# Ten gate buffers, all gates fetched within their step, and TensorE's block limits four instructions later

## The chip, the cores and the metric

The kernel runs on one core of a Trainium2 chip. Its five engines each work through a queue of their own in order: TensorE (PE, with weight loads listed apart as PEld), VectorE (DVE), ScalarE (ACT), GpSimd (POOL), and SyncE (SP), which here does nothing but issue DMAs. [...] The metric is the device time of one execution in microseconds (us); lower is better.

## The reference

One layer on an image x of shape (2, 128, 256, 256), all in float32: halo attention over windows, then a mixture of experts for each pixel, each with a normalisation before it and a residual around it.

```python
x = x + conv_attention(ln_over_channels(x))   # q, k, v by W_qkv; 8x8 windows look at 12x12 keys,
                                              # only every second row and column of them counts
t = tokens(x)
h = ln(t)
p = softmax(h @ router_w + router_b)          # 8 experts
top_p, top_i = top_k(p, 2); top_p /= top_p.sum()
out = einsum(h, expert_w) + expert_b          # all 8 experts
x = image(t + sum over the 2 chosen of top_p * out[top_i])
```

## The kernel before

**Steps.** The image is cut into strips of 8 rows, 32 a picture, 64 in all. The mask leaves only keys of one parity, so a strip falls into four planes (row parity by column parity) that attend separately. Each of the 256 planes is one step `n` of the loop at the end of the kernel; strip `i` and plane `pl` come from `divmod(n, 4)`. Seven more steps drain the pipeline. The scheduler's own ordering is off there: instructions run on each engine in the order in which the loop writes them, and generators (`score`, `attn`, `ahead`, `norm`, `outp`, `rout`) are advanced by `next` to interleave stages.

**What a step does.** It attends plane `n` (`scores` L462, `attend` L503, `out_project` L546), projects plane `n + 1` (`project` L400), and, a strip behind, runs the experts on 512 pixels. The experts are themselves spread over three steps: in one step the norms and the router of a group of pixels are computed; in the next its gates are written to DRAM (`spread` L648: gT to gd) and fetched back, each broadcast over 128 partitions; in the one after that they are multiplied in and the products made. `new` is the group whose gates are fetched in this step, `nxt` the one multiplied, `ex` the one whose products finish.

**Gates.** For each expert `e`, `fetch(e, eng)` (L680) takes a buffer `gb` of 128 x 512 from a ring, lets the engine `eng` touch its first column (a memset on DVE, L688, or a copy on ACT, L686), and issues the DMA on SP (L689). The touch makes one engine wait until the buffer's last reader is done, and the DMA then waits for that engine. `times(e, eng)` (L701, L705) multiplies the centred pixels `xs` by the gate into `xe`: 0 to 4 and 6 on DVE, 5 and 7 on POOL. `product(e)` (L711, L714) adds `xe` times the expert's weights into `acc`; `end` (L718, L720) adds `acc` to the pixels. `means` (L696, L699) makes `xs` from the pixels and `sb`, which `fetch_means` (L691, L694) brings.

**TensorE in a step**, in its order: 32 small matmuls with `keys` (L474) and 128 with `kcol` (L491), that is the scores; `pu` (L408), `pv` (L350), `pk` (L423), `pq` (L445) for the next plane; products of experts 4, 6, 7, 5 (L714, eight matmuls, since each product is two); 16 with `ones` (L512) and 128 with `vwin` (L522), that is the attention; the sums for the norms (L580, 32); products 0, 1, 2 (six matmuls), `po` (L550), product 3. Every matmul has a weight load, so that is 736 instructions. `pq` needs the PSUM buffer that `pu` had, which DVE frees with `uT` (L413).

**Alignment.** At the start of every full step TensorE gets an `addr_align` (L823): its next instruction is placed at `BLOCK - FIRST_LIMIT` = 161 in a block of 256 instructions, with no-ops as padding (they show on PEld's sequencer at L823, 32 a step). So the first block limit of a step comes 95 instructions after its start, and two more follow at every 256.

**SP in a step**, before: gates 5 and 7 of the group fetched in the step before (their touches on ACT), gd twice, vrows (values of the next plane, L369), rb (L665, the reciprocal deviation that `ln1` on POOL needs, L276), sb (L694), vwin in two halves (L381, `take_values`, which reads vrows back), gates 0, 1, 2, xt (L115, an image row pair ahead), gate 3, the output (L750, `store`), gate 4, the borders, gate 6.

**DVE in a step**: the router (L613 to L645), gT (L651), uT, the shifts (L392, L397), xs, six gate multiplications, `acc` to pixels (L720), sT, rc, rT, o for the attention (L532 to L542), the transposed sums plg (L589), the deviations (`rstd`, L232 to L239, with two activations on ACT between L235 and L238; then L596, L598), and `po` to pixels (L555). **POOL**: `behind` (L709, waits for DVE's last gate), gate 5, `ln1`, every fourth step `halo` (L250), gate 7.

Of the kernel before, what the change touches and what calls it, by code (L numbers as in the profile page):

```python
# [11 lines left out]
F32 = mybir.dt.float32  # L12
# [5 lines left out]
P = 128  # L18
# [25 lines left out]
KR, KC = 6, 10  # L44
NK = KR * KC
SLOT = 64
BLOCK, FIRST_LIMIT = 256, 95
NU = 9


# [1 line left out]
def kernel(  # L52
# [16 lines left out]
    nc = tc.nc  # L69
# [8 lines left out]
    NT = CH // P  # L78
# [7 lines left out]
    gates = ctx.enter_context(tc.tile_pool(name="gates", bufs=2))  # L86
# [18 lines left out]
    def load_x(i, k, paced=False):  # L105

        if i >= len(strips):
            return
        b, s = strips[i]
        if k == 0:  # L110
            xt[i] = xpool.tile([P, R, W], F32, tag="xt", name=f"xt{i}")
        r = s * R + 2 * k
        if paced:
            nc.scalar.copy(xt[i][:, 2 * k, 0:1], onesm[:, 0:1])
        nc.sync.dma_start(xt[i][:, 2 * k : 2 * k + 2, :], x[b, :, r : r + 2, :])  # L115
# [248 lines left out]
    def send_values(n, sent):  # L364

        i, pl = divmod(n, 4)
        for part, vr in sent:
            for k, at, m in runs(i, part):
                nc.sync.dma_start(  # L369
                    vrows[pl][1 : PC + 1, at : at + m, :],  # L370
                    vr[:, k - part[0] : k - part[0] + m],
                )

    def take_values(n):

        for half in range(2):
            src = vrows[n % 4][half * HP * 8 : half * HP * 8 + KC].rearrange("c r d -> (c r) d")
            src = src.unsqueeze(1)
            dims = [list(d) for d in src.ap]
            dims[1] = [8 * KR * P, HP]  # L380
            nc.sync.dma_start(  # L381
                vwin[n % 2][half * SLOT : half * SLOT + NK],
                bass.AP(src.tensor, src.offset, dims),
            )
# [77 lines left out]
    def scores(n, state):  # L462


        qs, kk, au = state["qs"], state["kk"], state["au"]
        turn = place(n // 4, 0) // 2
        att = ps_att.tile([P, 4, 512], F32, tag="att", name=f"att{n}")
        sc = att[:, :, 0:HQ]
        for w in range(2):
            for half in range(2):  # L470
                rows = slice(half * SLOT, (half + 1) * SLOT)
                for h in range(HEADS):
                    hp = slice(h * DH, (h + 1) * DH)
                    nc.tensor.matmul(  # L474
                        sc[rows, h].rearrange("p (t w z) -> p t w z", w=2, z=16)[:, :, w],
                        lhsT=keys[hp, turn, w],
                        rhs=au[hp, half * NP + w : (half + 1) * NP : 2].rearrange(
                            "p t a s -> p t (a s)"
                        ),
                        start=(w == 0),  # L480
                        stop=False,
                    )
        for t in range(HP):
            if t == HP // 2:
                yield
            for half in range(2):
                rows = slice(half * SLOT, (half + 1) * SLOT)
                m0 = 2 * (half * HP + t)
                for h in range(HEADS):
                    hp = slice(h * DH, (h + 1) * DH)  # L490
                    nc.tensor.matmul(  # L491
                        sc[rows, h, 32 * t : 32 * t + 32],
                        lhsT=kk[hp, half * HP + t, :],
                        rhs=qs[hp, m0 : m0 + 2].rearrange("p m a s -> p (m a s)"),
                        start=False,
                        stop=(t == HP - 1),
                    )
        pT = work.tile([P, HEADS, HQ], F32, tag="pT", name=f"pT{n}", bufs=1)
        nc.scalar.activation(pT, att[:, :, 0:HQ], AF.Exp)  # L499
        state.update(att=att, pT=pT)  # L500
        yield
# [166 lines left out]
    def to_all(gd, j):  # L668

        return gd[j * NT : (j + 1) * NT].rearrange("r k -> (r k)").partition_broadcast(P)  # L670

    class Experts:
# [7 lines left out]
        def fetch(self, e, eng):  # L680


            nm = "_".join(str(v) for v in (*self.at, e))
            self.gb[e] = gates.tile([P, NT * P], F32, tag="gb", name=f"gb{nm}", bufs=8)
            if eng is nc.scalar:
                eng.copy(self.gb[e][:, 0:1], onesm[:, 0:1])  # L686
            else:
                eng.memset(self.gb[e][:, 0:1], 0.0)  # L688
            nc.sync.dma_start(self.gb[e], to_all(self.gd, e))  # L689
# [55 lines left out]
    to_store = []  # L745

    def store(i, k):
        b, s = strips[i]
        r = s * R + 2 * k
        nc.sync.dma_start(out[b, :, r : r + 2, :], xt[i][:, 2 * k : 2 * k + 2, :])  # L750
        if k == R // 2 - 1:
            xt.pop(i)
# [4 lines left out]
    n_planes = 4 * len(strips)  # L757
# [45 lines left out]
    gated, ex, nxt = None, NoExperts(), NoExperts()  # L803
    last = ctile([P, 1], "last")
    pool, dve = nc.gpsimd, nc.vector

    ET = mybir.EngineType
    with tc.manual_schedule(engines={ET.PE, ET.DVE, ET.Activation, ET.Pool, ET.SP}):
        for n in range(n_planes + 7):
            i, pl = divmod(n, 4)  # L810
            score, attn, outp, ahead, norm, rout = none, none, none, none, none, none
            if n < n_planes:
                score = scores(n, states[n])
                attn = attend(n, states[n])
                outp = out_project(n, states[n])
            if n + 1 < n_planes:
                states[n + 1] = {}
                ahead = project(n + 1, states[n + 1])

            if 6 <= n < n_planes:
                nc.tensor.addr_align(BLOCK, offset=BLOCK - FIRST_LIMIT)  # L823


            next(score, None)
            new, row = NoExperts(), None
            if gated and gated[0]:
                rout = route(*gated[0], *gated[2])
            next(rout, None)  # L830
            nxt.fetch(5, nc.scalar)
            for _ in rout:
                pass
            next(score, None)
            next(ahead, None)
            nxt.fetch(7, nc.scalar)
            if gated:
                f, c, made = gated
                gd = spread(f, c, made[0], f"_{n}")
                new = Experts(*f, gd) if f else new  # L840
            if n + 1 < n_planes:
                send_values(n + 1, states[n + 1]["sent"])
            if gated and c:
                row = (*c, fetch_rstd(gd, f"_{n}"))
            next(ahead, None)
            if n + 1 < n_planes:
                states[n + 1]["shift"]()
            next(ahead, None)
            next(ahead, None)
            for e in (4, 6, 7, 5):  # L850
                ex.product(e)


            f = (i - 1, pl) if 0 < i <= len(strips) else None
            c = row_at(n)
            if f or c:
                norm = norms(f, c, f"_{n}")
            next(norm, None)
            next(attn, None)
            nxt.means()  # L860
            new.fetch_means()
            if n + 1 < n_planes:
                take_values(n + 1)
            for e in (0, 1, 2, 3):
                nxt.times(e, dve)
            new.fetch(0, dve)
            for e in (4, 6):
                nxt.times(e, dve)
            new.fetch(1, dve)
            ex.end()  # L870
            new.fetch(2, dve)
            next(attn, None)
            next(attn, None)


            ex = nxt
            next(norm, None)
            load_x((n + 9) // 4, (n + 9) % 4, paced=True)
            new.fetch(3, dve)
            while to_store:  # L880
                store(*to_store.pop())
            next(ahead, None)
            ex.product(0)
            made = next(norm, None)
            ex.product(1)
            ex.product(2)
            new.fetch(4, nc.scalar)
            nxt.behind(6)
            nxt.times(5, pool)
            if row:  # L890
                ln1(*row, pool)
            if pl == 3 and i + 2 < len(strips):
                halo(i + 2)
            nxt.times(7, pool)
            if n + 2 < n_planes:
                borders(n + 2)
            next(outp, None)
            ex.product(3)
            next(outp, None)
            new.fetch(6, dve)  # L900
            gated, nxt = (f, c, made) if made else None, new
            states.pop(n, None)

# [58 lines left out]
```

## Time and profile before

| What | us |
|---|---|
| median of 3 runs (lowest, highest) | 4416.81 (4413.12, 4420.5) |
| the profiled execution | 4415.92 |
| its span, first to last instruction | 4414.1 |
| start to the first of the 256 full steps | 29 |
| first steps with the experts not yet running | 114 (29 to 143) |
| steady steps | 4177 (143 to 4320) |
| draining steps | 94 (4320 to 4414) |
| TensorE busy in the steady part | 4084 of 4177, granted clock 1.00 |
| DVE busy in the steady part | 3700 |
| ACT, POOL busy in the steady part | 1399, 1055 |
| mean share of the 16 DMA engines in the steady part | 0.77 |

A line of the timeline has the start in us from the beginning of the span, the duration in us, the engine (with a q for its sequencer, which issues DMAs), the line of the kernel, the operation, what is written and read, the shape, and how many instructions were merged; in brackets stand the engine's idle time before the first of them and what ended it. "issue" there means that the engine waited for nothing that the profile shows. A line of the waits says who waited for whom: total in us, times, longest in us. A line of the windows begins with the stretch and its length, then busy us and instructions of PE, PEld, DVE, ACT and POOL, the granted TensorE clock, the share of the DMA engines and GB/s. A queue line has packets, MB and the share of 16 engines' time; q1 carries the kernel's transfers and q8 the instructions themselves. Matmuls are pipelined: a matmul of 512 columns is listed with some 0.6 us, but the next one starts 0.43 us after it, so starts are the better measure.

### The profile page before, as it was taken

What the parts mean: (1) busy time and instruction counts of PE and PEld (TensorE: products, weight loads), DVE (VectorE), ACT (ScalarE), POOL (GpSimd) and SP (SyncE); (2) the same over time, 40 slices, a digit from 0 to 9 for tenths busy, and PEclk for the clock granted to TensorE, in tenths of its full rate; (3) what the DMA queues carried; (4) which work ended last, traced back from release to release, by engine and by line L of the source; (5) the groups of instructions that cost most, each with busy time, mean ns of one, the idle gap of its engine ahead of it and who ended that gap; (6) DMA issues with size and microseconds to landing.
All of it is one profiled execution on the core that took longest, in us unless ns stands there. A gap on an engine that the chain in (4) does not pass through costs nothing. (4 is left out here: it accounts for less than half of the span.)

```text
span 4414.1 us, 224656 instructions
## 1 busy us (share of the span) xinstructions
PE 4254.2 (96%) x94273; PEld 2453.1 (56%) x94273; DVE 3844.2 (87%) x11850; ACT 1455.9 (33%) x3774; POOL 1092.5 (25%) x1126
## 2 busy tenths in 40 slices
PE   7899999999999999999999999999999999999987
PEld 4555555555555555555555555555555555555553
DVE  5788889888898988898888889988888888888877
ACT  3333333333333333333333333333333333333321
POOL 1122222222222222222222222222222222222211
PEclk9999999999999999999999999999999999999998
DMA  4677777777787777777878777777778777777865
GB/s 121 201 246 229 244 232 241 246 234 233 233 242 232 242 238 235 244 234 243 243 233 243 231 242 232 243 239 239 242 229 244 238 236 233 232 232 239 243 195 183
DMA packets 824580, 1022.19 MB, mean 232 GB/s; under 512 B 137634, under 2 KB 409634, under 8 KB 823594
## 3 DMA queue, kind: packets, MB, share of 16 engines
q1 hardware_dynamic: 822864, 1007.52, 74.6%
q8 instruction: 769, 12.60, 1.2%
q14 instruction: 217, 1.78, 0.1%
q10 hardware_dynamic: 730, 0.29, 0.0%
HBM read 863.78 MB, written 143.75 MB: 228 GB/s over the span
## 5 line engine op out<-in xcount | busy, mean ns | idle before, releaser
L714 PE MATMUL acc<-xe,ew 128*128 128x512 f32 x4096 | 1935.8, 602 | 66.7 <-issue 44.9
L714 PEld LDWEIGHTS acc<-xe,ew 128*128 128x128 f32 x4096 | 759.2, 190 | 1001.6 <-issue 931.2
L705 DVE TENSOR_TENSOR xe<-xs,gb 128x512 f32<-128x512 f32 x1536 | 951.0, 687 | 12.3 <-DMA gb<-gd 2.2
L709 POOL COPY last<-xe 128x1 f32<-128x1 f32 x256 | 47.0, 184 | 3119.1 <-DVE gb L688 3109.9
L705 POOL TENSOR_TENSOR xe<-xs,gb 128x512 f32<-128x512 f32 x512 | 650.8, 1272 | 2.5 <-PE acc L714 1.6
L276 POOL TENSOR_TENSOR xn<-xt,rb 128x512 f32<-128x512 f32 x249 | 374.0, 1502 | 171.5 <-DMA rb<-gd 165.4
L491 PE MATMUL att<-qs,kcol 32*64 32x32 f32 x32768 | 396.9, 226 | 4.8 <-issue 4.7
L491 PEld LDWEIGHTS att<-qs,kcol 32*64 32x64 f32 x32768 | 394.4, 131 | 6.3 <-issue 5.8
L522 PEld LDWEIGHTS att<-pT,vwin 64*32 64x32 f32 x32768 | 348.0, 105 | 37.5 <-issue 0.4
L522 PE MATMUL att<-pT,vwin 64*32 64x32 f32 x32768 | 343.3, 200 | 0.2 <-issue 0.2
L350 PEld LDWEIGHTS pv<-wt,xn 128*128 128x128 f32 x2048 | 270.5, 192 | 127.4 <-issue 80.1
L434 ACT COPY kcol<-pk 128x560 f32<-128x560 f32 (+2 forms) x344 | 318.9, 927 | 52.4 <-PE pk L423 49.0
L499 ACT ACTIVATE pT<-att 128x1024 f32<-128x1024 f32 x256 | 261.9, 1023 | 221.3 <-PE att L491 220.7
L532 DVE STREAM_TRANSPOSE sT<-att 128x512 f32<-128x512 f32 x256 | 183.5, 717 | 133.4 <-PE att L522 124.1
L445 PE MATMUL pq<-xn,wt 128*128 128x512 f32 x512 | 272.8, 614 | 23.4 <-DVE uT L413 21.4
L408 PE MATMUL pu<-xn,wrel 128*128 128x512 f32 x512 | 293.0, 654 | 0.0
L574 ACT ACTIVATE sq<-xt 128x512 f32<-128x512 f32 x505 | 291.8, 629 | 0.0
L397 DVE STREAM_TRANSPOSE au<-auT 128x512 f32<-128x512 f32 x256 | 272.5, 1064 | 9.0
L550 PE MATMUL po<-o,wt 128*128 128x512 f32 x512 | 265.1, 599 | 8.2 <-DVE o L542 5.8
L350 PE MATMUL pv<-wt,xn 128*128 128x128 f32 x2048 | 271.3, 275 | 0.9 <-issue 0.9
L423 PE MATMUL pk<-xn,wt 128*128 128x512 f32 (+2 forms) x528 | 263.4, 581 | 2.4 <-issue 1.3
L474 PEld LDWEIGHTS att<-au,keys 32*64 32x64 f32 x8192 | 117.2, 132 | 227.7 <-PE po L550 183.5
(2696 smaller groups left out, 4884.0 us busy)
## 6 DMA issues: line engine op xcount, KB each, us to landing
gb<-gd SPq DMA_DIRECT2D x2048, 256.0 KB, 5.7
vwin<-vrows SPq DMA_DIRECT2D x512, 240.0 KB, 5.4
xt<-in_x_dram SPq DMA_DIRECT2D x256, 256.0 KB, 6.4
sb<-gd SPq DMA_DIRECT2D x256, 256.0 KB, 4.2
out_dram<-xt SPq DMA_DIRECT2D x256, 256.0 KB, 6.0
rb<-gd SPq DMA_DIRECT2D x249, 256.0 KB, 3.4
vrows<-vr SPq DMA_DIRECT2D x168, 256.0 KB, 4.0
vrows<-vr SPq DMA_DIRECT2D x160, 128.0 KB, 3.6
```

Of the source, the lines that this page charges most:

```text
L276: eng.tensor_tensor(xn[i % 2][:, :, :, k, 1 : PC + 1], ln1_src(i, k).rearrange("p (y j x) -> p y x j", y=2, x=2), rb.rearrange("p (y j x) ...
L350: nc.tensor.matmul(pv[:, j * P : (j + 1) * P], lhsT=xp[:, k, 1 : PC + 1], rhs=wv, start=True, stop=True,)
L397: nc.vector.transpose(au.rearrange("p m a s -> p a s m"), auT[n % 2])
L408: nc.tensor.matmul(pu, lhsT=wrel, rhs=inner, start=True, stop=True)
L434: nc.scalar.copy(places[:, 1 : NP - 1], windows(new[:, :, KC - 3 :], 0, NP - 2))
L445: nc.tensor.matmul(pq, lhsT=wq, rhs=inner, start=True, stop=True)
L491: nc.tensor.matmul(sc[rows, h, 32 * t : 32 * t + 32], lhsT=kk[hp, half * HP + t, :], rhs=qs[hp, m0 : m0 + 2].rearrange("p m a s -> p (m a ...
L522: nc.tensor.matmul(av[hp, half, 32 * t : 32 * t + 32], lhsT=vv[rows, t, hp], rhs=pT[rows, h, 32 * t : 32 * t + 32], start=True, stop=True,)
L550: nc.tensor.matmul(po, lhsT=wo, rhs=state["o"].rearrange("p f z -> p (f z)"), start=True, stop=True)
L574: nc.scalar.activation(sq, src, AF.Square)
L705: eng.tensor_tensor(self.xe[e], self.xs, self.gb.pop(e), ALU.mult)
L714: nc.tensor.matmul(self.acc, lhsT=ew[:, e, :], rhs=self.xe.pop(e), start=(e == 0), stop=not self.xe)
```

## The change

Gates get ten buffers instead of eight. Gates 5 and 7, which were fetched at the beginning of the following step with touches on ACT, are fetched at the end of the step of their group, with touches on DVE, as is gate 4's; so all eight of a group are fetched in one step. The fetches, the two halves of `take_values`, the image load and the store are put in another order, and the first fetch comes after two gate multiplications rather than four. Gate 3's touch stands before the attention's transposes rather than after them. `FIRST_LIMIT` goes from 95 to 99, so TensorE's step starts at slot 157 of a block and each limit comes four instructions later in the step.

SP's order after it: gd twice, vrows, rb, sb, gate 0, vwin's first half, gate 1, xt, gate 2, gate 3, vwin's second half, the output, gates 4, 6, 5, 7, the borders.

```diff
--- before.py
+++ after.py
@@ -44,7 +44,7 @@
 KR, KC = 6, 10
 NK = KR * KC
 SLOT = 64
-BLOCK, FIRST_LIMIT = 256, 95
+BLOCK, FIRST_LIMIT = 256, 99
 NU = 9
 
 
@@ -371,9 +371,9 @@
                     vr[:, k - part[0] : k - part[0] + m],
                 )
 
-    def take_values(n):
-
-        for half in range(2):
+    def take_values(n, halves=(0, 1)):
+
+        for half in halves:
             src = vrows[n % 4][half * HP * 8 : half * HP * 8 + KC].rearrange("c r d -> (c r) d")
             src = src.unsqueeze(1)
             dims = [list(d) for d in src.ap]
@@ -681,7 +681,7 @@
 
 
             nm = "_".join(str(v) for v in (*self.at, e))
-            self.gb[e] = gates.tile([P, NT * P], F32, tag="gb", name=f"gb{nm}", bufs=8)
+            self.gb[e] = gates.tile([P, NT * P], F32, tag="gb", name=f"gb{nm}", bufs=10)
             if eng is nc.scalar:
                 eng.copy(self.gb[e][:, 0:1], onesm[:, 0:1])
             else:
@@ -828,12 +828,10 @@
             if gated and gated[0]:
                 rout = route(*gated[0], *gated[2])
             next(rout, None)
-            nxt.fetch(5, nc.scalar)
             for _ in rout:
                 pass
             next(score, None)
             next(ahead, None)
-            nxt.fetch(7, nc.scalar)
             if gated:
                 f, c, made = gated
                 gd = spread(f, c, made[0], f"_{n}")
@@ -859,32 +857,39 @@
             next(attn, None)
             nxt.means()
             new.fetch_means()
-            if n + 1 < n_planes:
-                take_values(n + 1)
-            for e in (0, 1, 2, 3):
+            for e in (0, 1):
                 nxt.times(e, dve)
             new.fetch(0, dve)
+            if n + 1 < n_planes:
+                take_values(n + 1, (0,))
+            for e in (2, 3):
+                nxt.times(e, dve)
+            new.fetch(1, dve)
+            load_x((n + 9) // 4, (n + 9) % 4, paced=True)
             for e in (4, 6):
                 nxt.times(e, dve)
-            new.fetch(1, dve)
+            new.fetch(2, dve)
             ex.end()
-            new.fetch(2, dve)
+            new.fetch(3, dve)
+            if n + 1 < n_planes:
+                take_values(n + 1, (1,))
+            while to_store:
+                store(*to_store.pop())
             next(attn, None)
+            new.fetch(4, dve)
             next(attn, None)
+            new.fetch(6, dve)
+            new.fetch(5, dve)
 
 
             ex = nxt
             next(norm, None)
-            load_x((n + 9) // 4, (n + 9) % 4, paced=True)
-            new.fetch(3, dve)
-            while to_store:
-                store(*to_store.pop())
             next(ahead, None)
             ex.product(0)
             made = next(norm, None)
+            new.fetch(7, dve)
             ex.product(1)
             ex.product(2)
-            new.fetch(4, nc.scalar)
             nxt.behind(6)
             nxt.times(5, pool)
             if row:
@@ -897,7 +902,6 @@
             next(outp, None)
             ex.product(3)
             next(outp, None)
-            new.fetch(6, dve)
             gated, nxt = (f, c, made) if made else None, new
             states.pop(n, None)
 
```

## The prediction

> **What bounds the kernel now.** I read the page first, then TensorE step by step in the timeline, the waits, the DMA queues, and at last the order in which SP issues.
>
> ```profile
> PE 4254.2 (96%) x94273; PEld 2453.1 (56%) x94273; DVE 3844.2 (87%) x11850; ACT 1455.9 (33%) x3774; POOL 1092.5 (25%) x1126
> ...
> q8 instruction: 769, 12.60, 1.2%
> ```
>
> TensorE is the bound. The 256 full steps (from one L474 to the next) take 16.80 us on average over steps 10 to 244. The fastest agree to the nanosecond, and there TensorE never pauses:
>
> ```profile
> 1620.10:1636.37 16.27, 16.27 (x370) 9.53 (x369) 14.67 (x44) 5.54 (x14) 4.71 (x5) 1.00 0.75 230
> ```
>
> So 0.52 us of a step, some 124 us over those 235 steps, is all that can be won from TensorE's pauses. Taking each matmul's start against the one before it, minus the usual spacing at its place in the step, puts them in four places: 62.3 us at the second matmul of L714's group of eight (101 steps), 45.5 us at L445 (pq), 7.5 us inside L491 (17 steps), 1.3 us inside L522. What ends the first two:
>
> ```profile
> 1155.28 0.59 PE L714 MATMUL acc<-xe,ew 128*128 128x512 f32 x1
> 1156.87 3.16 PE L714 MATMUL acc<-xe,ew 128*128 128x512 f32 x7 [1.00 <-issue]
> ...
> 1775.67 1.13 PE L445 MATMUL pq<-xn,wt 128*128 128x512 f32 x2 [0.42 <-DVE uT L413]
> ```
>
> The first is no wait on data. q8 brings 16 KB packets, three a step, and a step holds 768 TensorE instructions: a packet is a block of 256. Counting from the aligned start, the first limit falls 95 instructions in, at L491's 16th matmul (64 for L474, then 31). The second, at 351, is the second matmul of L714 (348 come before L714, then load, matmul, load). The third, at 607, is L522's 106th. These are exactly the places of the three pauses called "issue". Over 1154.4 to 1155.4 us the queues show
>
> ```profile
> q1 hardware_dynamic: 126, 0.22, 58.2%
> q8 instruction: 1, 0.02, 6.0%
> ```
>
> That packet starts at 1154.60, 4.1 us after the first limit was passed, and TensorE goes on 2.27 us after its start. No stalled step resumes sooner than 2.2 us after a packet's start. The packet for the second limit starts 3.1 us after the first limit in the median (2.2 to 4.2), and more DMAs in flight at that moment delay it: 2.70 us with four, 2.97 with five, 3.23 with six, 3.80 with seven, 0.37 us for each.
>
> SP shows why so much is in flight:
>
> ```profile
> 1150.89 3.88 SPq L689 DMA_DIRECT2D gb<-gd  x2
> 1154.87 1.71 SPq L659 DMA_DIRECT2D gd<-gT  x2
> 1156.63 1.05 SPq L369 DMA_DIRECT2D vrows<-vr  x2
> 1158.69 0.32 SPq L665 DMA_DIRECT2D rb<-gd  x1
> ```
>
> Gates 5 and 7 go out a step late, at 1.17 and 4.70 us after the step's start (medians), each behind an ACT copy, and SP's later issues queue behind them: gT is ready at 3.85, but gd leaves at 5.12.
>
> The pause at pq starts on DVE and POOL:
>
> ```profile
> 1768.49 0.99 DVE L235 SCALAR_TENSOR_TENSOR u__103_33034<-u__103_33034,epsc 128x8 f32<-128x8 f32 x1
> ...
> 1768.19 1.27 POOL L705 TENSOR_TENSOR xe<-xs,gb 128x512 f32<-128x512 f32 x1
> ...
> POOL xn L276 <- DMA rb<-gd: 165.4, 129, 29.2
> ```
>
> L235 usually takes 0.17 us. Here it ends 22 ns after POOL's multiplication, as in each of its 103 long cases. POOL is late because ln1 (L276) waits for rb. DVE is then late by 0.48 us on average in 122 such cases, uT has 0.25 us to spare (ends at 4.37, pq free at 4.66), and pq waits for the rest.
>
> **The change part by part.** FIRST_LIMIT 99 moves each limit four instructions: to L491's 18th matmul and L522's 108th (about 30 ns each), and to the fourth matmul of L714's group, two spacings of 0.43 later, 0.86 us. The padding stays within three blocks, so its no-ops cost what they cost now.
>
> *Second limit.* With every packet at its old time, only what exceeds 0.86 remains: 9.4 us in 25 steps, a gain of 53. The DMAs should also be earlier. From rb to the next step's drain there are fourteen transfers of about 256 KB at some 0.8 us each (4 MB in 12.5 busy us a step). They now start at 8.47 and saturate the engines to about 4 us of the next step. I expect rb at about 7.1 and the last gate at 16, so the backlog ends near 2 to 2.5, about two transfers less in flight at the first limit (0.7 us). I take a gain of 60. Bounds: 62, and 12 if instead two more are in flight.
>
> [...]
>
> *Third limit.* The stretch from the second limit to the third shrinks from 4.22 to 3.36 us, and the third packet starts 1.31 us after the second limit in the median (0.69 to 2.18), needing 2.2 more. If packets keep their absolute times, the pauses there grow from 1.3 to 6.2 us. If the packet moves the full 0.86 with the limit, they grow to 39.8 in 96 steps. Which? Where the previous packet came early, the next started as little as 0.02 us before the second limit's matmul, against 1.06 after it at least where that matmul had stalled: the sequencer runs up to 1.1 us ahead, which covers 0.86. I take a loss of 6; bounds 5 and 38.
>
> *First limit.* It moves 0.02 us and must be met within 4.2 us of the third. I take a gain of 2 from 7.5; bounds 7.5 gained and 10 lost, since SP now issues faster right after the third limit.
>
> *Gates, DVE and ACT.* Eight gates a step as before; three ACT copies of 0.18 us go (ACT is 33% busy, nothing on the path) and three DVE memsets of 59 ns come. A memset between two L705 costs nothing: 22 plus 579 ns from start to start against 602 without. Two come together after L542, and one now stands between L598 and L555; I allow 0.06 us, on the 0.25 spare. Gates 0 and 1 now reuse buffers that POOL read at 10.4 to 15.1 of the step before, so DVE finds them free at 7.7; the other six were last read by DVE earlier in its own queue. Behind these memsets stand sT and rstd: if one did wait, attention and then po would. Ten buffers cover the extra lifetime of two gates.
>
> *SP's queue.* Without gates 5 and 7 in front, gd leaves at about 4.0 instead of 5.12, vrows follow vr at 5.1 and rb goes at about 7.1 instead of 8.47. vwin's first half waits for vrows as now, but gate 0 passes it and fills the idle stretch before 10.5. The second half goes about 2 us later; it lands some 5.4 later, early in the next step, and L522 reads it at 9.5. xt moves ahead and still finds its ACT copy (7.75) done. The store finds L720 done at 10.9.
>
> *pq.* With rb earlier POOL ends at about 14.38, where L235 starts at 14.34, so most collisions go. In the quarter of steps with halo (L250, 0.62 us) POOL ends at 15.0: 62 times (0.70 minus 0.25) is 28 us. With 5 for the rest and 3 for the memsets, 45.5 becomes 36. Gain 10; bounds 30 gained, 15 lost.
>
> Sum: 60 - 6 + 2 + 10 = 66 us. The profiled execution took 4415.9 (span 4414.1, 1.8 around it), which gives 4349.9; the median shown is 0.9 higher, so **4350**. All pauses gone would be about 4298.
>
> **Rivals.**
> *The pause moves to the third limit (slower).* rb, sb and gate 0, now at 7 to 8.5 us, are in flight just when the third packet must start. It starts at 7.76 now; against the third limit at 10.67 it may start at 8.47. The other terms' gain of 72 is used up at 0.29 us a step, a start at 8.76. At 8.95 the pause is 0.48 in each of 245 steps, 118 lost against 72: 4462. For it: only 0.7 us of room. Against: the engines are only 38 to 69% busy at 5 to 7.5 now, and gate 7 leaves that stretch.
> *Half given back.* The packet does move with the limit (38 lost), rb comes no earlier (0), the second limit gains 53: 4402.
> *DVE becomes the bound.* Its work spaced back to back is 15.94 us a step, with collisions 16.20, against TensorE's 16.27. At 0.2 us for each of three memsets it is 16.80, today's step: 4417. Against: the free memset above.
> *It doesn't do what it says.* If the added waits change TensorE's count before L714, the limit doesn't land two matmuls on; only the DMA order acts, about 25 us: 4392.
>
> **How the numbers follow.** Forecast 0.58, half given back 0.15, limit misplaced 0.07, DVE bound 0.06, third limit 0.14. A difference under 0.2% (8.8 us) can't be told from none. The first three lie below 4408: faster 0.80; same 0.06; slower 0.14. The range 4300 to 4412 leaves out the slower case, most of the DVE case and a sliver below; the forecast's own range is 4300 to 4385.
>
> **What would show it.** Right: L714 in one piece of eight in most steps and pauses at its fourth matmul rare; q8's packets starting about 2 to 3 us after a step's start; gd right behind gT; POOL's wait for rb nearly gone; pq's waits only every fourth step. Wrong: an "issue" gap inside L522 in most steps, DVE memsets that wait, or a step floor other than 16.27.

## The result, and the profile after

| | us |
|---|---|
| before, median of the runs on the same chip (lowest, highest) | 4418.66 (4413.12, 4424.38) |
| after, median of 4 runs (lowest, highest) | 4632.52 (4620.21, 4636.44) |
| ratio after to before, with its 95% interval | 1.0479 (1.0455 to 1.0503) |
| span of the profiled execution, before and after | 4414.1 and 4630.3 |
| mean granted TensorE clock over the span, before and after | 0.992 and 0.980 |
| mean length of a step (steps 10 to 244), before and after | 16.80 and 17.68 |

The change made the kernel 4.8% slower; 4350 had been forecast, with a range up to 4412. The mean step is 0.885 us longer, which is 208 us over 235 steps, and nearly all of the 214 us between the medians.

The page after, engines and instruction queue:

```profile
PE 4311.1 (93%) x94273; PEld 2511.4 (54%) x94273; DVE 3816.6 (82%) x12618; ACT 1391.0 (30%) x3006; POOL 1089.4 (24%) x1126
...
q8 instruction: 769, 12.60, 1.2%
```

TensorE is still the bound, has the same 94273 matmuls and the same 769 packets of instructions, and the step without pauses is as long as before (the window line of one such step):

```profile
1622.27:1638.54 16.27, 16.27 (x369) 9.50 (x368) 14.76 (x50) 5.65 (x13) 4.67 (x5) 1.00 0.75 196
```

So neither DVE's three memsets nor more work on TensorE explains the loss: it lies in pauses. The waits after, for the places that mattered before (total us, times, longest us):

```profile
PE att L491 <- issue: 166.4, 175, 4.1
...
POOL xn L276 <- DMA rb<-gd: 114.0, 49, 30.4
...
PE att L522 <- issue: 48.4, 56, 1.9
...
PE acc L714 <- issue: 18.2, 34, 1.3
```

The pauses at L714 and at pq that the prediction set out to remove did shrink, and POOL waits less often for rb (49 times, 129 before). But L491, where the first limit of a step lies, now has the largest wait of TensorE's matmuls. Taking starts against starts as in the prediction (steps 10 to 244; us in total, with the number of steps over 30 ns; a matmul's usual spacing at its place is taken off):

| place | before | after | difference |
|---|---|---|---|
| first limit, in L491 | 7.5 (17) | 195.6 (191) | +188 |
| second limit, in L714 | 62.4 (101) | 25.3 (55) | -37 |
| third limit, in L522 | 1.3 (13) | 58.6 (87) | +57 |
| pq, L445 (both matmuls) | 45.5 | 6.6 | -39 |
| wider spacing at L408 and L350 | 1.1 | 39.3 | +38 |
| sum | | | +208 |

One step shows the first row. It starts at 1195.09. TensorE's timeline first, around the third limit, then around the first limit of the following step:

```profile
1205.89 1.15 PE L522 MATMUL att<-pT,vwin 64*32 64x32 f32 x107
1207.57 0.32 PE L522 MATMUL att<-pT,vwin 64*32 64x32 f32 x21 [0.53 <-issue]
...
1213.81 0.37 PE L491 MATMUL att<-qs,kcol 32*64 32x32 f32 x17
1215.50 1.34 PE L491 MATMUL att<-qs,kcol 32*64 32x32 f32 x111 [1.33 <-issue]
```

107 matmuls, then a pause, then 21: the third limit is at the 108th. 17 matmuls, then a pause, then 111: the first limit is at the 18th. Both are where the prediction's count puts them. SP's queue in the same stretch:

```profile
1201.94 0.35 SPq L665 DMA_DIRECT2D rb<-gd  x1
1202.42 0.37 SPq L694 DMA_DIRECT2D sb<-gd  x1
1203.62 0.32 SPq L689 DMA_DIRECT2D gb<-gd  x1
1204.43 0.34 SPq L381 DMA_DIRECT2D vwin<-vrows  x1
1204.86 0.39 SPq L689 DMA_DIRECT2D gb<-gd  x1
1205.31 1.28 SPq L115 DMA_DIRECT2D xt<-in_x_dram  x1
1206.64 0.90 SPq L689 DMA_DIRECT2D gb<-gd  x2
1207.64 0.39 SPq L381 DMA_DIRECT2D vwin<-vrows  x1
```

Eight transfers went out in the 5.6 us before the third limit (1207.57), six of them (four gates, half of vwin, xt) of the kind that went out at this limit or behind it before; the last line is already behind it. The instruction packet starts at 1212.96, 5.4 us after the limit; the queues from 1212.5 to 1213.5 are full:

```profile
q1 hardware_dynamic: 324, 0.31, 101.2%
q8 instruction: 1, 0.02, 6.1%
```

TensorE goes on 2.54 us after that packet's start; the shortest such time at any limit of steps 10 to 244 (without 123 to 130, which have other counts of matmuls) is 2.17 us here and was 2.18 before, the prediction's 2.2. Over all steps, the packet now starts 4.53 us after the third limit in the median, 2.19 before. It never starts sooner than 0.84 us after that limit in those steps before, 1.94 after; that it is asked for at the limit is read from these times. The first limit of the next step comes 6.45 us after the third (median before, from start to start), so by these numbers a packet that starts more than 6.45 less 2.2, that is 4.25 us, after the third limit should stop TensorE. It paused after 166 of the 167 packets that started later than that, and after 25 of the 67 others.

### The profile page after: what moved, and what is told of

Same layout as the page of the kernel before. It is cut to its first block, busy times and chain, and to the rows that moved or that the text cites. A ratio compares the mean times of both kernels' runs of the same rounds, so it can differ in the third digit from the quotient of the medians.

```text
span 4630.3 us, 224762 instructions
## 1 busy us (share of the span) xinstructions
PE 4311.1 (93%) x94273; PEld 2511.4 (54%) x94273; DVE 3816.6 (82%) x12618; ACT 1391.0 (30%) x3006; POOL 1089.4 (24%) x1126
## 3 DMA queue, kind: packets, MB, share of 16 engines
q1 hardware_dynamic: 822864, 1007.52, 75.6%
## 5 line engine op out<-in xcount | busy, mean ns | idle before, releaser
L714 PE MATMUL acc<-xe,ew 128*128 128x512 f32 x4096 | 1925.4, 601 | 36.9 <-issue 18.2
L714 PEld LDWEIGHTS acc<-xe,ew 128*128 128x128 f32 x4096 | 759.0, 190 | 965.4 <-issue 895.5
L491 PE MATMUL att<-qs,kcol 32*64 32x32 f32 x32768 | 433.3, 227 | 166.8 <-issue 166.4
L491 PEld LDWEIGHTS att<-qs,kcol 32*64 32x64 f32 x32768 | 413.8, 133 | 185.3 <-issue 184.1
L522 PEld LDWEIGHTS att<-pT,vwin 64*32 64x32 f32 x32768 | 351.1, 105 | 91.8 <-issue 54.5
L522 PE MATMUL att<-pT,vwin 64*32 64x32 f32 x32768 | 352.2, 200 | 48.8 <-issue 48.4
L350 PEld LDWEIGHTS pv<-wt,xn 128*128 128x128 f32 x2048 | 290.9, 205 | 141.0 <-issue 92.1
L408 PE MATMUL pu<-xn,wrel 128*128 128x512 f32 x512 | 315.7, 701 | 0.0
L413 DVE STREAM_TRANSPOSE uT<-pu 128x512 f32<-128x512 f32 x256 | 179.2, 700 | 146.6 <-PE pu L408 145.3
L350 PE MATMUL pv<-wt,xn 128*128 128x128 f32 x2048 | 289.2, 287 | 0.8 <-issue 0.8
L445 PE MATMUL pq<-xn,wt 128*128 128x512 f32 x512 | 263.2, 595 | 3.8 <-issue 2.3
```

The costliest lines, as they stand in the source:

```text
L350: nc.tensor.matmul(pv[:, j * P : (j + 1) * P], lhsT=xp[:, k, 1 : PC + 1], rhs=wv, start=True, stop=True,)
L408: nc.tensor.matmul(pu, lhsT=wrel, rhs=inner, start=True, stop=True)
L491: nc.tensor.matmul(sc[rows, h, 32 * t : 32 * t + 32], lhsT=kk[hp, half * HP + t, :], rhs=qs[hp, m0 : m0 + 2].rearrange("p m a s -> p (m a ...
L522: nc.tensor.matmul(av[hp, half, 32 * t : 32 * t + 32], lhsT=vv[rows, t, hp], rhs=pT[rows, h, 32 * t : 32 * t + 32], start=True, stop=True,)
L714: nc.tensor.matmul(self.acc, lhsT=ew[:, e, :], rhs=self.xe.pop(e), start=(e == 0), stop=not self.xe)
```

## The experiments

Each of them was also measured for its pauses (us as in the table above), for the median time from the third limit to the start of the packet, and for how many transfers SP issued in the 4 us before that limit. The times of e2, e3, e4, e5, e6, e8 and e9 are of one execution each, the others medians. The kernel before that ran beside them had a median of 4405.39 (e1, e2, e4, e6), 4418.88 (e3, e7, e8) or 4408.05 (e5, e9, e10).

| kernel | time | first | second | third | pq | packet after third limit | issued in 4 us |
|---|---|---|---|---|---|---|---|
| before | 4418.66 | 7.5 | 62.4 | 1.3 | 45.5 | 2.19 | 3.5 |
| after | 4632.52 | 195.6 | 25.3 | 58.6 | 6.6 | 4.53 | 5.6 |
| e1: limit 99 alone | 4374.84 | 13.4 | 8.2 | 19.5 | 44.4 | 2.18 | 3.5 |
| e2: after with limit 95 | 4631.62 | 176.2 | 78.4 | 42.2 | 1.4 | 4.53 | 5.8 |
| e4: five and seven in step | 4413.77 | 46.1 | 48.2 | 12.0 | 6.9 | 3.74 | 5.5 |
| e6: zero to three early | 4680.74 | 141.1 | 182.6 | 1.2 | 14.3 | 4.25 | 4.9 |
| e3: after, gates behind attention | 4540.28 | 128.7 | 62.8 | 16.1 | 11.4 | 4.03 | 3.9 |
| e8: after, values late | 4513.68 | 101.2 | 56.7 | 39.5 | 11.3 | 4.28 | 5.0 |
| e7: after, two gates then hold | 4425.24 | 43.9 | 49.8 | 15.5 | 27.0 | 3.95 | 4.0 |
| e5: before, gate 0 early | 4513.93 | 99.7 | 79.3 | 2.6 | 22.2 | 4.01 | 4.5 |
| e9: after, nothing in front | 4537.79 | 0.3 | 61.3 | 38.1 | 140.9 | 2.00 | 2.1 |
| e10: limit 99, gate 7 behind means | 4374.5 | 4.4 | 23.4 | 6.9 | 50.6 | 2.00 | 3.2 |

The theory after the result: the new order of SP's issues puts transfers in front of the third limit, the packet asked for there is served behind them, and TensorE stops at the next first limit. The rivals: the moved limit does it; more gates in flight from the end of the step do it.

**The limit alone (e1), and the order alone (e2).**

```diff
--- before                                   (e1)
-BLOCK, FIRST_LIMIT = 256, 95
+BLOCK, FIRST_LIMIT = 256, 99
--- after                                    (e2)
-BLOCK, FIRST_LIMIT = 256, 99
+BLOCK, FIRST_LIMIT = 256, 95
```

Of e1:

> The kernel before with FIRST_LIMIT 99 and nothing else. Theory (an instruction packet is served behind the transfers that SP issued before it was asked for, so the new issue order delays the packet asked for at the third limit): the order is that of before, so packets keep their times; pauses at the second limit fall from 62 to some 9 us, those at the third grow from 1 to 6 to 40 us; 4375 to 4400 us. Rival (the moved limits themselves cost the time, the stretch from second to third limit being 0.86 us shorter): 4500 us or more, with pauses inside L522 in most steps.

Of e2:

> The changed kernel with FIRST_LIMIT back at 95. Theory: the transfers in front of the third limit's packet stay, so some 200 us of pauses inside L491 stay; pauses at the third limit shrink, those at the second grow; 4580 to 4660 us. Rival (the moved limits): back to 4450 us or less, with no pauses inside L491.

e1 took 4374.84 us (4370.49 to 4381.2): 0.9934 of the time before (0.9911 to 0.9957). Of the limits, the waits of TensorE in e1 show two:

```profile
PE att L522 <- issue: 11.0, 33, 1.2
...
PE att L491 <- issue: 9.4, 19, 1.1
```

The second limit's, in L714, comes below them now. Start to start, the second limit's pauses fell by 54 us and the third's rose by 18. e2, a single execution, took 4631.62, the time of the change itself, with 176 us at the first limit. So the loss is there without the moved limit: it comes from the order and the buffers, and the limit on its own gains.

**Which half of the order (e4, e6).** e4 is the kernel before with ten buffers and gates 5 and 7 fetched at the end of their own step; e6 is the kernel before with only the new order of gates 0 to 3, vwin's halves, xt and the store. Both have limit 95.

```diff
--- before                                   (e4)
-            ... bufs=8)
+            ... bufs=10)
...
-            nxt.fetch(5, nc.scalar)
...
-            nxt.fetch(7, nc.scalar)
...
             new.fetch(6, dve)
+            new.fetch(5, dve)
+            new.fetch(7, dve)
--- after                                    (e6)
-BLOCK, FIRST_LIMIT = 256, 99
+BLOCK, FIRST_LIMIT = 256, 95
...
-            ... bufs=10)
+            ... bufs=8)
...
+            nxt.fetch(5, nc.scalar)
...
+            nxt.fetch(7, nc.scalar)
...
-            new.fetch(4, dve)
-            new.fetch(6, dve)
-            new.fetch(5, dve)
...
-            new.fetch(7, dve)
...
+            new.fetch(4, nc.scalar)
...
+            new.fetch(6, dve)
```

Of e4:

> The kernel before with ten buffers and gates 5 and 7 fetched at the end of their own step behind gate 6, the other order and limit 95 kept. Theory: gates 0 to 2 still leave after vwin, so few transfers stand before the third limit; pauses inside L491 stay under 60 us; 4370 to 4460 us. Rival (fetching all gates within the step gives the backlog, wherever the first ones stand): 4550 us or more, pauses inside L491 near 200 us.

Of e6:

> The kernel before with only the issue order of gates 0 to 3, vwin's halves, xt and the store taken from the change; eight buffers, gates 4 to 7 and limit 95 as before. Theory: more transfers stand before the third limit, its packet starts well over 3 us after it instead of 2.2, pauses inside L491 over 100 us; 4500 to 4640 us. Rival (gates 5 and 7 within the step make the backlog): 4380 to 4450 us.

e4 took 4413.77 and e6 4680.74 in one execution each, beside 4405.39. Gates 5 and 7 moved into their own step bring pq's gain (45.5 to 6.9) and give it back at the first limit (7.5 to 46.1): nothing is left. The new order of gates 0 to 3, vwin, xt and the store alone, with eight buffers, loses 275 us: neither the ten buffers nor the new place of gates 5 and 7 is needed for the loss. In e6 gates 5 and 7 still go out at the start of the step, and its second limit waits 183 us; e6's loss is larger than expected, and larger than that of the whole change.

**One gate in front (e5).** The kernel before, with gate 0 fetched behind two multiplications and in front of vwin, everything else as it was.

```diff
--- before                                   (e5)
             new.fetch_means()
+            for e in (0, 1):
+                nxt.times(e, dve)
+            new.fetch(0, dve)
             if n + 1 < n_planes:
                 take_values(n + 1)
-            for e in (0, 1, 2, 3):
+            for e in (2, 3):
                 nxt.times(e, dve)
-            new.fetch(0, dve)
```

> One transfer as a dose: the kernel before (limit 95) with gate 0 alone moved in front of vwin, into the idle stretch at some 9.4 us. Theory: it stands in front of the third limit's packet, which starts at 2.6 to 3.3 us after the limit instead of 2.2; pauses inside L491 grow from 8 to 15 to 60 us; 4410 to 4470 us. Rival (a transfer in an idle stretch is free, as the prediction had it): packet unchanged at 2.2 us, the backlog at the first limit shrinks by one transfer and the pauses at the second limit fall from 62 to some 40 us; 4380 to 4405 us.

4513.93, beside 4408.05. SP issues gate 0 at 10.03 us of the step in the median and vwin at 10.86 and 11.30, against 10.55 and 10.99 before; the third limit is at 11.24, against 10.91 before. The waits of e5:

```profile
POOL xn L276 <- DMA rb<-gd: 189.3, 154, 30.4
...
PE att L491 <- issue: 79.3, 109, 3.2
...
PE acc L714 <- issue: 56.9, 115, 1.1
```

L491 waits for "issue" 109 times, 11 times in the same view of the kernel before: with one gate in SP's idle stretch the packet starts 1.82 us later (2.19 to 4.01). The loss, 106 us, is beyond what was expected. So a gate in that stretch is not free, though the prediction priced it at nothing. Its place differs from the change, though: here gate 0 goes out 1.2 us before the third limit, in the change at 8.66 us of the step, 3.0 us before it, with gates 1 and 2, half of vwin and xt between, and in the step shown gate 3 too.

**Nothing in front (e9).** The change, with every gate, vwin and xt held on DVE until `rc` of the attention is done, which is behind the third limit. What waits, waits on the touches in DVE's own order.

```diff
--- after                                    (e9)
             new.fetch_means()
-            for e in (0, 1):
+            for e in (0, 1, 2, 3, 4, 6):
                 nxt.times(e, dve)
+            ex.end()
+            next(attn, None)
             new.fetch(0, dve)
             if n + 1 < n_planes:
-                take_values(n + 1, (0,))
-            for e in (2, 3):
-                nxt.times(e, dve)
+                take_values(n + 1)
             new.fetch(1, dve)
             load_x((n + 9) // 4, (n + 9) % 4, paced=True)
-            for e in (4, 6):
-                nxt.times(e, dve)
             new.fetch(2, dve)
-            ex.end()
             new.fetch(3, dve)
-            if n + 1 < n_planes:
-                take_values(n + 1, (1,))
...
-            next(attn, None)
```

> The changed kernel (limit 99, all gates in the step) with every gate, vwin and xt held behind the attention's first DVE part, so that SP issues nothing between sb and the third limit. Theory: the third limit's packet starts within 1.6 us and the pauses inside L491 fall from 200 to under 10 us; the same transfers then stand in front of the first limit's packet, which starts more than 4.3 us after it, so that the pauses at L714's fourth matmul grow from 25 to over 100 us; 4480 to 4650 us. Rival (something else in the order holds TensorE inside L491): pauses there stay over 60 us.

4537.79, beside 4408.05. Its waits:

```profile
POOL xn L276 <- DMA rb<-gd: 348.8, 231, 29.4
PEld pq L445 <- DVE uT L413: 271.4, 238, 1.7
...
PE pq L445 <- DVE uT L413: 81.4, 178, 0.9
...
PE acc L714 <- issue: 43.0, 84, 1.4
```

No wait of L491 for "issue" is left in that view, and start to start no step pauses there (0.3 us in all): the packet starts 2.00 us after the limit. That is the cause shown from the other side, although the packet was expected within 1.6 us. The packet asked for at the next first limit starts 4.42 us after it (3.12 before), as expected, but the pauses at L714 grow to 61 us only, not to over 100. The kernel is still slower than before, since everything held back now goes out later and the next step's rb with it (10.02 us against 8.47), so POOL and pq wait in nearly every step (141 us at pq) and L235 in most.

**Between the two (e3, e7, e8).** In e3 gates 1, 2, 3 and xt are held behind `rc` and only gate 0 and vwin's first half stay in front; in e7 gates 0 and 1 stay in front, and vwin goes behind; in e8 only vwin's first half goes to the second, behind the limit.

```diff
--- after                                    (e3)
-            for e in (2, 3):
+            for e in (2, 3, 4, 6):
                 nxt.times(e, dve)
+            ex.end()
+            next(attn, None)
             new.fetch(1, dve)
...
--- after                                    (e7)
             new.fetch(0, dve)
-            if n + 1 < n_planes:
-                take_values(n + 1, (0,))
             for e in (2, 3):
                 nxt.times(e, dve)
             new.fetch(1, dve)
-            load_x((n + 9) // 4, (n + 9) % 4, paced=True)
             for e in (4, 6):
                 nxt.times(e, dve)
+            ex.end()
+            next(attn, None)
             new.fetch(2, dve)
-            ex.end()
+            if n + 1 < n_planes:
+                take_values(n + 1)
+            load_x((n + 9) // 4, (n + 9) % 4, paced=True)
             new.fetch(3, dve)
-            if n + 1 < n_planes:
-                take_values(n + 1, (1,))
...
--- after                                    (e8)
             new.fetch(0, dve)
-            if n + 1 < n_planes:
-                take_values(n + 1, (0,))
...
             if n + 1 < n_planes:
-                take_values(n + 1, (1,))
+                take_values(n + 1)
```

Of e3:

> The changed kernel (limit 99) with gates 1, 2, 3 and xt touched and issued after the attention's first DVE part (rc), so that in front of the third limit stand only rb, sb, gate 0 and vwin's first half. Theory (the third limit's packet waits for what SP issued before it): its packet starts at about 2.5 us after the limit instead of 4.5 and the pauses inside L491 fall from 200 to under 40 us; 4370 to 4440 us, the rest being a larger backlog at the first limit. Rival (the pauses come from having all eight gates in one step, whenever issued): stays above 4550 us.

Of e7:

> A version meant to keep the gain and lose the loss: limit 99, all gates within the step, gates 0 and 1 in the idle stretch after sb, then nothing until the attention's first DVE part is done, and after it gate 2, both vwin halves, xt, gate 3, the output and the rest. Theory: third limit's packet within 2 us, pauses inside L491 under 15 us, rb early so that pq hardly waits (45 down to 10 to 20 us), pauses at second and third limit together 20 to 50 us; 4320 to 4370 us. Rival (the backlog only moves on to the first limit): pauses at the second limit over 60 us, 4390 us or more.

Of e8:

> The changed kernel (limit 99) with vwin's first half moved back next to the second, gates 0 to 3 and xt staying early. If what counts is the time that the transfers in front take on the engines (a vwin half some 1.7 us in 512-byte pieces, a gate some 0.65 us, read off the spacing of landings): the third limit's packet comes 1 to 1.7 us sooner, near 3.2 us, and the pauses inside L491 fall from 200 to 40 to 80 us; 4420 to 4500 us. If only the number of transfers counts (1.1 us each by the two traces): one fewer, but xt and gate 2 move up in its place, packet above 4 us and pauses above 120 us; 4550 us or more.

e3 took 4540.28, beside 4418.88, where at most 4440 was expected; e7 took 4425.24 (4416.79 to 4438.25), 1.001 of the time before (0.9995 to 1.0026), where at most 4370 was expected. Both miss for the same reason. Holding transfers back delays the tail of the queue, and the tail delays the next step's head: rb goes out at 8.92 in e3 and 8.66 in e7 rather than at 7.12. gd leaves as early as in the change (3.88 and 3.92, against 3.87) but takes 4.5 and 4.4 us to land, not 2.8, and rb waits for it. So what was left in front came right before the limit (gate 0 at 10.44 in e3; gates 0 and 1 at 10.25 and 10.99 in e7) rather than three microseconds ahead of it. Fewer were in front (3.9 and 4.0 in 4 us), but the packet started 4.03 and 3.95 us after the limit all the same. e8 took 4513.68, between what the two readings of "in front" had called for: engine time at most 4500, number of transfers at least 4550. Its packet, at 4.28, fits the second reading, its pauses (101 us inside L491) neither; it decides for neither. By the mean times of their packets in the change's trace, half of vwin takes the 16 engines 1.06 us and a gate 0.86, not the 1.7 and 0.65 of the first reading, so that reading called for too much.

**A version for use (e10).** The kernel before with limit 99; gate 7 goes from the front of the step to behind sb, and vwin waits behind gate 0's touch, behind L720, so that little is issued in the last microsecond before the third limit.

```diff
--- before                                   (e10)
-BLOCK, FIRST_LIMIT = 256, 95
+BLOCK, FIRST_LIMIT = 256, 99
...
-            nxt.fetch(7, nc.scalar)
...
             new.fetch_means()
-            if n + 1 < n_planes:
-                take_values(n + 1)
-            for e in (0, 1, 2, 3):
+            nxt.fetch(7, nc.scalar)
+            for e in (0, 1, 2, 3, 4, 6):
                 nxt.times(e, dve)
+            ex.end()
             new.fetch(0, dve)
-            for e in (4, 6):
-                nxt.times(e, dve)
+            if n + 1 < n_planes:
+                take_values(n + 1)
             new.fetch(1, dve)
-            ex.end()
```

> Limit 99 in the kernel before, gate 7 fetched behind sb instead of in front of gd (so gd, rb and the means go early), gates 0, 1, 2 touched behind L720 and vwin behind gate 0, gate 5 and the rest as before. Theory: rb near 7.1 us, so pq's waits fall from 45 to 10 to 20 us; in front of the third limit only rb, sb and gate 7, packet near 2.2 us and pauses inside L491 under 20 us; pauses at the second and third limit 10 and 25 us; 4325 to 4370 us. Rival (gate 7 behind sb counts like any transfer in front of the third limit): pauses inside L491 over 60 us, 4390 us or more.

4374.5 (4369.41 to 4376.25), 0.9921 of the time before (0.9897 to 0.9946). That is just above the 4370 expected. The second and third limits together do what was expected (23.4 and 6.9, for 10 and 25), as does the first (4.4). pq's part did not come (50.6): rb left at 8.15, not at 7.1. gd went out early, at 3.96, but landed 3.8 us later, against 2.8 in the change, and rb waits for it. e1 and e10 are both faster than the kernel before and than the change; their intervals overlap, and e1 is one number in the source.

## Why the prediction was wrong

**The step that failed is "First limit".** It reads "I take a gain of 2 from 7.5; bounds 7.5 gained and 10 lost, since SP now issues faster right after the third limit." What was measured there is a loss of 188 us. The step considered what SP issues *after* the third limit; what SP issues *before* it decides. Two claims carried the error there:

- In the paragraph on SP's queue, "gate 0 passes it and fills the idle stretch before 10.5" was priced at nothing. Up to six transfers moved in front of the third limit, and their effect on the packet asked for at that limit was worked out nowhere. e5 puts it at 1.82 us for one gate, 1.2 us ahead of the limit; e2 and after put it at 2.34 us for all of them.
- The prediction had a price, "0.37 us for each", taken at the *first* limit, with four to seven transfers in flight. At the third limit the kernel before had 3.5 issues in 4 us, and 2.1 more cost 2.34 us, or 1.1 each. And it was never carried from the one limit to the other, though the distance was to be had: 6.45 less 2.2, against 2.19, left 2.06 us to spare in the median. Even at 0.37 us each, six transfers use up 2.2 us; the question would have been asked.

The half clock behind the pauses (38 us, the last section) had no term either.

**Second limit.** The moved limit was right: 53 us by packets at old times, 54 in e1. In the change it brought 37, not 60: the packet at the first limit starts 2.92 us after it (3.12 before, from the start of the limit's matmul), not 0.7 us sooner. The last gate goes out 18.1 us after its step's start in the median, not at 16, so it falls into the next step, and that step is itself held up in L491. With limit 95 the new order even adds 16 us there (e2).

**Third limit.** Predicted 6 lost, bounds 5 and 38. In e1 it lost 18, inside them; in the change 57. The room there was read too small: from start to start the stretch between the second and third limit goes from 4.50 to 3.65 us, not from 4.22 to 3.36, and the third limit is at 10.91 before, not 10.67. The rival "the pause moves to the third limit" named this place and a cause (rb, sb and gate 0 in flight when its packet must start) at 118 us. It was half as large, and no run tested that cause: in e9, where rb leaves only at 10.02, the third limit still has 38 us. A late packet one limit on, at the first limit of the next step, which no rival named, cost more than three times what the third limit did. Limit 99 adds 16 us at the third limit (42 without it, in e2) and takes 53 off the second.

**pq.** Predicted 10 gained (bounds 30 gained, 15 lost), measured 39, beyond the bound. rb does leave at 7.12 and gd at 3.87, as worked out (7.1 and 4.0); L235's long cases fall from 103 to 22. The loss of 28 that was allowed for the steps with halo did not come. But e4 and e9 point to a trade: where the queue ends early, rb is early and transfers stand in front of the limit (e4); where it ends late, neither holds (e9).

**Gates, DVE and ACT.** Right: the memsets cost nothing. From the start of L542 to that of L589, the stretch into which two of them fell, it was 616 ns before and 625 after, the fastest steps are unchanged at 16.27, and no touch waits.

**Signs.** Of the signs named, "gd right behind gT" and "POOL's wait for rb nearly gone" came; "pauses at its fourth matmul rare" came in part (55 steps); and the sign against it, "an 'issue' gap inside L522", came in 87 of 235 steps, not in most. q8's packets "starting about 2 to 3 us after a step's start" did not come: the first one starts at 4.39 (3.80 before). A gap in L491 was not on the list.

**What stays open.** What exactly must stand in front of the packet. The number of issues in 4 us does not order the kernels (3.9 gives 4.03 in e3, 3.5 gives 2.19 before). Nor does the landing of the last one in front, as far as the traces give it (7.3 us after the limit in the change, 5.1 before, 4.7 in e7 with the packet at 3.95). Nor does the load on the DMA engines in the microsecond before the limit: 0.61 before and 0.70 in e10 go with 2.19 and 2.00, 0.62 in e5 and 0.68 in e3 with 4.01 and 4.03.

Step by step the traces say more. Count the gates, halves of vwin, xt and outputs that SP issued in the last 2 us before the third limit, over steps 10 to 244 of all twelve kernels: with none the packet starts 1.88 us after the limit in the median (388 steps), with one 2.16 (458), with two 3.97 (941), with three or more 4.32 (1033). It shows within the kernel before alone: 1.98 with one half of vwin in front (91 steps), 2.38 with both (55), 3.22 with both and a gate (27). It is not the whole rule: one gate alone goes with 1.90 in e10 (187 steps) and 3.80 in e5 (36). Whether the packet waits in an engine's queue, for the memory, or for something else was not tried.

## What to carry to other kernels

Here the instructions came in 769 packets of 16 KB, three a step, and took 1.2% of the time of the 16 DMA engines, of which the data took 75.6% (after). In such a kernel, write down for every block limit when its packet is asked for, what is issued just before that, and how much time there is until the next limit. Moving transfers into an "idle" stretch of an issuing queue was not free here: over the twelve kernels, with two of them issued in the 2 us before the third limit the packet started 3.97 us after it in the median, with none 1.88. Take the spare time of each limit (here 2.06 us at the first) as a resource that an edit can use up, also at the limits that show no pause today. A one-number shift of the limits to places where the gap behind them is long can be had without touching the transfers: here it gained 0.66%, and e10, with a new order besides, 0.79%, which the intervals do not tell apart.

## What the runs showed of the hardware

**TensorE ran at half clock after some of its pauses.** The last row of the table of pauses is no wait: in 30 of the 235 steps after (none before), L408 and L350 are spaced at up to twice the usual distance. Step 217 in TensorE's timeline, and the windows over it (the third number from the end is the granted clock):

```profile
3852.04 0.37 PE L491 MATMUL att<-qs,kcol 32*64 32x32 f32 x17
3855.00 1.57 PE L491 MATMUL att<-qs,kcol 32*64 32x32 f32 x111 [2.58 <-issue]
3856.50 2.08 PE L408 MATMUL pu<-xn,wrel 128*128 128x512 f32 x2
```

```profile
3852.00:3854.00 2.00, 0.41 (x38) 0.32 (x19) 1.82 (x8) 0.23 (x1) 0.00 (x0) 1.00 1.11 275
3854.00:3856.00 2.00, 1.00 (x94) 1.00 (x97) 1.15 (x6) 0.00 (x0) 0.00 (x0) 0.94 1.08 366
3856.00:3857.00 1.00, 1.00 (x40) 0.94 (x31) 0.00 (x0) 0.39 (x1) 0.00 (x0) 0.50 1.09 402
3857.00:3858.00 1.00, 1.00 (x2) 0.34 (x1) 0.00 (x0) 0.63 (x1) 0.00 (x0) 0.50 0.62 208
3858.00:3859.00 1.00, 1.00 (x4) 0.63 (x3) 0.39 (x1) 0.00 (x0) 0.00 (x0) 0.50 0.23 58
3859.00:3860.00 1.00, 1.00 (x8) 0.84 (x7) 0.93 (x4) 0.15 (x1) 0.00 (x0) 0.91 0.05 16
```

After 2.58 us of idleness the clock drops to 0.50, from some 3855.8 (0.94 over two microseconds is 0.24 us at half) to 3859.2 (0.91 over one is 0.18), that is 3.4 us, while TensorE is busy again. The two matmuls of `pu` then start 1.01 us apart rather than 0.53. The clock record of the trace has 31 stretches at 0.50 in these steps after, 30 of them 3.41 us long and one 6.83, and two of 3.41 us before, behind pauses of 1.97 and 2.22 us in L714. In the 30 steps the wider spacing costs 0.8 to 1.6 us each behind the pause, 38 us in all, 18% of the loss. The 30 pauses with it last 1.5 to 4.3 us; others of up to 2.2 us went without. What decides between them is not shown.

**Block limits cost far more here than the packets' own time.** The pauses at the three limits make 71 us before and 280 after, out of 4414 and 4630, by the table above, although the instruction packets take 1.2% of the DMA engines' time. In no step of the twelve kernels (123 to 130, which have other counts of matmuls, left out) does TensorE pass a limit sooner than 2.15 us after the start of its packet, and no two packets start within 3.2 us of each other.
